# A Perceiver layer on one core: nine products of constants at the start, and three gate/up steps of the second half done inside the self attention

## The chip, the cores and the metric

The kernel runs on one core of a Trainium2 chip. The metric is the device time of one execution in microseconds; less is better. The engines are named as the profile names them: PE (TensorE, products), PEld (its weight loads), DVE (VectorE), ACT (ScalarE), POOL (GpSimd) and SP (SyncE, which here only issues DMAs). Each engine works through its own queue in order and waits on semaphores of others.

## The reference

A layer works on 16 sequences of 64 rows of 1024 numbers (1024 rows in all), with a context of 1024 rows for each sequence. In short:

```
x = x + cross_attention(layernorm(x), ctx)      # 32 heads of 32, 8 key/value heads, Wq Wk Wv Wo
x = x + self_attention(layernorm(x))            # rotary embedding, biases, no output weights
x = x + ffn(layernorm(x))

def ffn(x):
    xq = int4_quant(x)                          # per row: mean |x|, round, clip to -8..7
    gate, up = xq @ ternary(w_gate), xq @ ternary(w_up)     # 1024 -> 2752
    inter = int8_quant(up * relu(gate)**2)      # per row: max |.|, round
    return inter @ ternary(w_down)              # 2752 -> 1024
```

`ternary(w)` is -1, 0 or 1 times the mean of |w|, so each weight matrix must be read once for its mean and again to be rounded.

## The kernel before, in words

The 1024 rows make eight tiles of 128 rows, numbered 0 to 7 (two sequences each). Almost all of on-chip memory is one tile named `arena`, of which the code hands out places by hand: `place(kb, shape)` is a view that begins `kb` KB into each partition. The order of all instructions on all queues is the order of the Python code (`manual_schedule`); nothing is moved by a scheduler. Waits follow from the places and PSUM banks that instructions share.

**Start (lines 135 to 282).** Constants are made; then 8 chunks of the first context half are loaded on SP's queue (L266) and of the key/value weights on ACT's queue (L267). After them come the rows `x`, the second context half and the query weights. `project_first` (L584) multiplies chunk after chunk: for each chunk two key products of 512 columns (L590) and four value products of 256 columns (L598). Then follow the layer norms, transposes and query products (L360), and the first pass over the feed-forward weights.

**Cross attention (most of the time).** 32 units, two for each sequence. Products for the next sequence's keys and values (L497, L508) are cut into pieces and called between the steps of a unit: they are "fillers", a list from which `fill(n)` takes the next n entries. Context loads are released by the products that used their places before. Meanwhile all three feed-forward weight matrices pass through the core twice (L636, L644).

**Self attention (from L1464).** A loop over `t` = 0 to 8 handles tile `t` (called `two`) and the tile before it (`last`). For each tile: scores (`by_key`, L972), copies to memory (L982), row maxima on DVE (`maxima`, `row`) that go through a small DRAM buffer and come back on all partitions (L1012, L1016), subtraction (L1021), exponentials on ACT (L1024), values and sums on PE (`values`, L1032 and L1043), copies (L1051, L1054), transposes back (`finish`, L1064 and L1067), and the residual added on POOL (L1080). The scores of tile `t` and the values of tile `t` - 1 use the same four PSUM banks, `w`. Then comes the quantisation of the tile for the feed-forward part (`quantize`): statistics on DVE (L187), a power on POOL (L193), normalisation (L179), mean of |x| (L1113), rounding, and a transposing DMA on SP (L1125) that makes `xqT[t]`. `factors3` (L1131, L1132) makes the two factors of a tile on POOL.

**Gate/up steps.** The 2752 columns are cut into 8 chunks of 344. Step (n, t) multiplies tile t by gate and up chunk n (`gate_up`, L1144): 2 x 8 products of 128x344 (L1151) into two banks. Numbers 0 to 7 are the chunks for tiles 0 to 3 (the first half), 8 to 15 the same chunks again for tiles 4 to 7 (the second half); 64 steps in all. With `scalar=True` ACT does the relu, the scaled copy and the square (L1159, L1161, L1162), otherwise ACT does the relu and DVE a fused product (L1165); POOL makes the last product (L1163 or L1168). `fetch(n)` loads chunk n of both matrices into one of four pairs of places, for n < 4 on SP's queue, else on POOL's (L1141). Numbers from 8 on use the first three pairs only, since the fourth lies where tile 4's results are put.

While cross attention's leftovers last, the fillers of the self-attention loop are projections (`project2`, L252); from `t` = 4 on they are the 32 steps of the first half, as L1480 to L1491 order them. The second half (from L1535) is a plain list of steps with other work hung on to positions in it (`beside`): the down weights' load (`fetch_down`), the quantisation of tile 7, that of the results (`quantize8`), and the down products of tiles 0 and 1 (`down`, L1213). The remaining down products end the kernel.

Of the kernel before, what the change touches and what calls it, by code (L numbers as in the profile page):

```python
# [11 lines left out]
F32 = mybir.dt.float32  # L12
BF = mybir.dt.bfloat16
# [36 lines left out]
def kernel(  # L50
# [82 lines left out]


    ident = const.tile([P, P], F32, name="ident")
    make_identity(nc, ident)
# [8 lines left out]
    for g in range(2):  # L145
        nc.vector.memset(pick[:, g, g : g + 1], 1.0)
    minus = const.tile([P, P], BF, name="minus")
    nc.vector.memset(minus, -1.0)
    bq_sb = const.tile([P, 8], F32, name="bq_sb")
# [944 lines left out]
    ]  # L1094
    wb_pairs = [(112, 114.6875), (117.375, 120.0625), (91.25, 122.75), (0, 2.6875)]
    relu_ring = Ring(125.4375, 192.25, 199.625)
# [37 lines left out]
    def fetch(n):  # L1134

        wbs[n] = []
        pair = wb_pairs[n % 4] if n < NCH else wb_pairs[(n - NCH) % 3]
        for i in range(2):
            q = place(pair[i], [KC, CW], F8)
            queue = nc.sync if n < 4 else nc.gpsimd  # L1140
            queue.dma_start(q.rearrange("p k o -> p (k o)"), ternary[i][n % NCH])  # L1141
            wbs[n].append(q)
# [90 lines left out]
    with tc.manual_schedule():  # L1233
# [234 lines left out]
        fill(2)  # L1468
        two, last = None, None
        for t in range(NT + 1):  # L1470
            two, last = (Tile2(t, w) if t < NT else None), two
# [4 lines left out]
            if t == NT // 2:  # L1476
                fill(len(fillers))
                for n in (2, 3):
                    fetch(n)
                steps = [(n, tt) for n in range(NCH) for tt in range(NT // 2)]  # L1480

                steps[:12] = [
                    (n, tt) for tiles in ((0, 1), (2,), (3,)) for n in range(3) for tt in tiles
                ]

                def beside(n, tt):
                    gate_up(n, tt, lambda i: four_tile(f"gu_{n}_{tt}_{i}"), scalar=True)
                    if tt == NT // 2 - 1 and n + 4 < NCH + 3:
                        fetch(n + 4)

                fillers += [lambda s=s: beside(*s) for s in steps]  # L1491
# [6 lines left out]
            if t == NT // 2:  # L1498
                fill(2)
                last.exponentials()  # L1500
# [6 lines left out]
            if last and t != NT // 2:  # L1507
                last.exponentials()
                fill()

# [24 lines left out]
        pieces = quantize(NT - 1)  # L1535
        steps = [(n, t) for n in range(NCH, 2 * NCH) for t in range(NT // 2, NT)]

        steps[:12] = [s for s in steps[:12] if s[1] < NT - 1] + [s for s in steps[:12] if s[1] == NT - 1]
        beside = {9 + 2 * i: step for i, step in enumerate(sum(map(quantize8, range(4)), []))}
        beside[0] = fetch_down  # L1540
# [3 lines left out]
        for t in range(2):  # L1544
            beside[20 + 8 * t] = lambda t=t: (down(t, 0), down(t, 1))
        more = None
        for i, (n, t) in enumerate(steps):
            if i == 2:
                ps_w_closed.close()
                more = ctx.enter_context(tc.tile_pool(name="ps_g", bufs=4, space=PSUM))  # L1550
            if more:
                gate_up(n, t, lambda j: more.tile([P, 512], F32, tag="g", name=f"g_{n}_{t}_{j}"))
            else:
                gate_up(n, t, lambda j: four_tile(f"gu_{n}_{t}_{j}"))
            if i in beside:
                beside[i]()
            if t == NT - 1 and n + 3 < 2 * NCH:
                fetch(n + 3)
        for t in range(2, NT):
# [74 lines left out]
```

## Time and profile before

| what | value |
|---|---|
| median of three runs | 1798.24 us (1792.51, 1798.24, 1798.41) |
| profiled execution | 1793.57 us |
| its span | 1791.80 us |
| PE busy | 1746.8 us (97%) |
| DVE, ACT, POOL busy | 1270.0, 922.3, 946.6 us |
| self attention's second half (first step to tile 7's last transposes) | 1522.85 to 1633.31 us |

The span runs from the first to the last instruction of one execution; the time of the execution has some 1.8 us more. In a list of waits, a line gives the waiting engine and line of code, what ended the wait, the total, how many times, and the longest. In a timeline a row gives the start and the duration in microseconds from the span's start, the engine, the line, the operation, and `x4` for four instructions drawn together; rows of one engine may overlap a little, since the next instruction begins before the last one's results are out. A product of 32-bit numbers counts as two instructions. The brackets at the end of a row say how long the engine was idle before it and what released it.

### The profile page before, as it was taken

Reading aid. Unit: us, or ns where it says so; the run is one execution under the profiler, and the core shown is the slowest. Engines: PE = TensorE matmul, PEld = TensorE weight load, DVE = VectorE, ACT = ScalarE, POOL = GpSimd, SP = SyncE. Lnnn points to the kernel's source line nnn. Section 1 sums busy time; section 2 is a strip of 40 time slices with the busy share of each in tenths; the row PEclk is TensorE's granted clock in tenths of the full one; section 3 lists DMA queues with packets and bytes.
Section 4 is the critical chain, followed back from the end, with each engine's and each line's share of the span. In section 5 each row is a group of like instructions: output and inputs, shape, how many; then the busy total and the mean of one; then the engine's idle time right before and its main releaser. Section 6 shows DMA issues by size and latency. Waiting matters only on the chain.

```text
span 1791.8 us, 29303 instructions
## 1 busy us (share of the span) xinstructions
PE 1746.8 (97%) x12184; PEld 1119.1 (62%) x12184; DVE 1270.0 (71%) x1520; ACT 922.3 (51%) x1004; POOL 946.6 (53%) x564
## 2 busy tenths in 40 slices
PE   8999999999999999999999999999999999899999
PEld 5778566666667666666666666664446454566654
DVE  4343678778888888887888888889554258775564
ACT  1563566555777777776776775544201122564100
POOL 1000447576676676677577577576503433555530
PEclk9999999999999999999999999999999999999999
DMA  9575466557766776776785784551430024354534
GB/s 357 178 245 187 177 193 200 172 148 186 198 218 183 232 230 184 226 236 169 226 250 162 231 237 129 148 168 57 99 127 14 1 48 88 75 139 128 123 73 108
DMA packets 99093, 293.35 MB, mean 164 GB/s; under 512 B 41808, under 2 KB 50960, under 8 KB 84240
## 3 DMA queue, kind: packets, MB, share of 16 engines
q1 hardware_dynamic: 85232, 220.10, 36.4%
q0 software_dynamic: 12576, 69.28, 19.4%
q8 instruction: 96, 1.57, 0.4%
q10 hardware_dynamic: 1152, 2.10, 0.3%
q14 instruction: 37, 0.30, 0.1%
HBM read 264.38 MB, written 19.20 MB: 158 GB/s over the span
## 4 chain that ended last, share of the span: by engine, by line
PE 72%; DVE 12%; DMA 8%; ACT 3%; issue 2%; POOL 2%; SPq 0%; DVEq 0%; ACTq 0%; POOLq 0%
PE p L508 13%; PE p L497 12%; PE t L690 6%; PE o L752 6%; PE k L252 4%; PE q L252 4%; PE d L1213 4%; PE g L1151 4%; DVE arena L733 3%; DMA arena<-in_ctxT 3%; PE z L508 3%; PE wo L854 3%; PE q L360 3%; DVE arena L709 2%; PE v L421 2%; PE gu L1151 2%
## 5 line engine op out<-in xcount | busy, mean ns | idle before, releaser
L743 POOL TENSOR_TENSOR arena<-arena 128x1024 f32<-128x1024 f32 x188 | 497.7, 2647 | 72.7 <-ACT arena L734 62.2
L709 DVE TENSOR_TENSOR arena<-t,arena 128x512 f32<-128x512 f32 x384 | 261.2, 688 | 163.9 <-PE t L690 93.9
L733 DVE TENSOR_TENSOR arena<-arena 128x2048 f32<-128x2048 f32 x128 | 355.6, 2807 | 2.1 <-DMA arena<-tops 2.1
L734 ACT ACTIVATE arena<-arena 128x2048 f32<-128x2048 f32 x128 | 244.0, 1907 | 179.2 <-DVE arena L733 179.1
L508 PEld LDWEIGHTS p<-arena 128*128 128x128 f32 x2688 | 309.9, 192 | 34.0 <-issue 26.2
L702 ACT COPY arena<-t 128x1024 f32<-128x1024 f32 x256 | 253.1, 1009 | 137.4 <-DVE arena L706 61.7
L508 PE MATMUL p<-arena 128*128 128x128 f32 x2688 | 318.0, 277 | 0.0
L497 PE MATMUL p<-arena 128*128 128x512 f32 x672 | 309.4, 602 | 8.3 <-DMA arena<-in_ctxT 8.2
L497 PEld LDWEIGHTS p<-arena 128*128 128x128 f32 x672 | 122.1, 191 | 152.5 <-issue 136.5
L740 POOL TENSOR_TENSOR arena<-arena 128x1024 f32<-128x1024 f32 x32 | 77.4, 2417 | 262.5 <-ACT arena L734 180.9
L690 PE MATMUL t<-arena 32*128 32x256 f32 x2048 | 146.6, 400 | 2.8 <-DVE arena L709 2.5
L1151 PEld LDWEIGHTS <-arena 128*128 128x128 bf16 x1024 | 98.7, 97 | 58.7 <-issue 5.0
L690 PEld LDWEIGHTS t<-arena 32*128 32x128 f32 x2048 | 93.0, 184 | 61.3 <-issue 32.6
L752 PE MATMUL o<-arena 128*32 128x256 f32 x2048 | 123.8, 382 | 0.4 <-DVE wmean L653 0.4
L252 PE MATMUL q<-arena 128*128 128x512 f32 x256 | 112.2, 594 | 0.0
L854 PE MATMUL wo<-arena 128*128 128x512 f32 x224 | 100.5, 598 | 5.7 <-ACT arena L845 4.8
L360 PE MATMUL q<-arena 128*128 128x256 f32 x448 | 100.5, 382 | 3.1 <-ACT arena L371 1.7
L913 POOL TENSOR_TENSOR arena<-arena 128x512 f32<-128x512 f32 x20 | 33.5, 1672 | 118.3 <-DVE arena L911 118.3
L360 PEld LDWEIGHTS q<-arena 128*128 128x128 f32 x448 | 83.7, 190 | 18.2 <-ACT arena L371 4.0
L752 PEld LDWEIGHTS o<-arena 128*32 128x32 f32 x2048 | 60.2, 109 | 53.4 <-ACT arena L640 6.8
L477 POOL DMA_DIRECT2D arena<-in_ctxT x70 | 70.4, 1064 | 30.1 <-PE z L508 16.0
L1151 PE MATMUL gu<-arena 128*128 128x344 fp8e4 x544 | 83.3, 311 | 2.4 <-DMA arena<-arena 1.9
(156 smaller groups left out, 2318.4 us busy)
## 6 DMA issues: line engine op xcount, KB each, us to landing
arena<-in_ctxT SPq DMA_DIRECT2D x56, 1024.0 KB, 10.6
arena<-in_ctxT POOLq DMA_DIRECT2D x42, 1024.0 KB, 10.7
arena<-tops SPq DMA_DIRECT2D x48, 512.0 KB, 4.9
arena<-in_wg SPq DMA_DIRECT2D x32, 688.0 KB, 5.0
arena<-in_wu SPq DMA_DIRECT2D x32, 688.0 KB, 5.0
arena<-in_wd SPq DMA_DIRECT2D x32, 688.0 KB, 8.2
arena<-in_ctxT POOLq DMA_DIRECT2D x28, 512.0 KB, 8.7
ternary<-arena SPq DMA_DIRECT2D x48, 172.0 KB, 7.2
```

The costliest lines, as they stand in the source:

```text
L252: nc.tensor.matmul(made[0], lhsT=lhsT(k), rhs=rhs(k), start=(k == 0), stop=(k == KC - 1))
L360: nc.tensor.matmul(ps, lhsT=weights[:, k, :], rhs=what[:, k, :], start=(start and k == 0), stop=(k == 3), skip_group_check=True,)
L497: nc.tensor.matmul(ps, lhsT=weights[:, k, :], rhs=what[:, k, :], start=(first and k == 0), stop=(k == 3), skip_group_check=True,)
L508: nc.tensor.matmul(ps[:, bass.ts(kt, P)], lhsT=what[:, k, bass.ts(kt, P)], rhs=weights[:, k, :], start=(first and kt == 0 and k == 0), sto ...
L690: nc.tensor.matmul(ws[jj // 2][:, jj % 2, a, :], lhsT=self.kT[rows, self.g, bass.ts(i * 2 + a, P)], rhs=two_tiles[self.b // 2 % 2][rows, s ...
L702: nc.scalar.copy(pt[:, 2 * mine : 2 * mine + 2], ws[mine])
L709: nc.vector.tensor_tensor(m, w[:, :, a], m, ALU.max)
L733: nc.vector.tensor_tensor(pt, pt, by.to_broadcast([P, 4, 2, 256]), ALU.subtract)
L734: nc.scalar.activation(pt, pt, AF.Exp)
L743: nc.gpsimd.tensor_tensor(acc, acc, pt[:, :, a], ALU.add)
L752: nc.tensor.matmul(self.po[bass.ts(jj, HD), 0:256], lhsT=self.v[:, kt, bass.ts(self.g * 4 + jj, HD)], rhs=self.pts[i][:, jj, a, :], start= ...
L1151: nc.tensor.matmul(ps[:, :CW], lhsT=xqT[t][:, k, :], rhs=wbs[n][i][:, k, :], start=(k == 0), stop=(k == KC - 1),)
```

## The change

1. At the start, a place of 512 numbers of 16 bits is filled with ones on DVE, and PE multiplies it nine times into a bank that nobody reads. The constant `minus`, which no instruction read, and its memset are gone.
2. Steps (8, 4), (9, 4) and (8, 5) of the second half become the last three fillers of the self-attention loop (`ahead`), with `scalar=True`, and are taken out of the second half's list.
3. The loop asks for one more filler at three places: ahead of tile 3's exponentials, and after the exponentials at `t` = 5 and `t` = 8.
4. The order of the first 16 steps of the first half changes: chunk 3's steps for tiles 0 to 2 come before the four steps of tile 3, which before stood three places earlier.
5. Numbers 11 and 15 of the chunks get a fifth pair of places of their own (where `xqT` of tiles 0 to 3 lay), so that a chunk is fetched four numbers ahead instead of three in the second half; fetch 11 is now issued in the loop.
6. The positions in the second half's list move by three (`quantize8` from 9 to 6, down products from 20 to 17).

```diff
+    idle = place(200, [512], BF)
+    nc.vector.memset(idle, 1.0)
+    ps = t_tile([P, 512], F32, "idle")
+    for _ in range(9):
+        nc.tensor.matmul(ps, lhsT=idle[:, :P], rhs=idle, start=True, stop=True)
...
-    minus = const.tile([P, P], BF, name="minus")
-    nc.vector.memset(minus, -1.0)
...
-    wb_pairs = [(112, 114.6875), (117.375, 120.0625), (91.25, 122.75), (0, 2.6875)]
+    wb_pairs = [(112, 114.6875), (117.375, 120.0625), (91.25, 122.75), (0, 2.6875), (176, 193.75)]
...
-        pair = wb_pairs[n % 4] if n < NCH else wb_pairs[(n - NCH) % 3]
+        pair = wb_pairs[4 if n % 4 == 3 and n > NCH else n % 4]
...
+        ahead = [(NCH, NT // 2), (NCH + 1, NT // 2), (NCH, NT // 2 + 1)]
...
-                steps[:12] = [
-                    (n, tt) for tiles in ((0, 1), (2,), (3,)) for n in range(3) for tt in tiles
+                steps[:16] = [(n, tt) for tiles in ((0, 1), (2,)) for n in range(3) for tt in tiles] + [
+                    (3, 0), (3, 1), (3, 2), (0, 3), (1, 3), (2, 3), (3, 3)
                 ]
+                steps += ahead
...
-                    if tt == NT // 2 - 1 and n + 4 < NCH + 3:
+                    if tt == NT // 2 - 1:
                         fetch(n + 4)
...
             if t == NT // 2:
-                fill(2)
+                fill(3)
                 last.exponentials()
...
             if last and t != NT // 2:
                 last.exponentials()
-                fill()
+                fill(2 if t in (NT // 2 + 1, NT) else 1)
...
-        steps[:12] = [s for s in steps[:12] if s[1] < NT - 1] + [s for s in steps[:12] if s[1] == NT - 1]
-        beside = {9 + 2 * i: step for i, step in enumerate(sum(map(quantize8, range(4)), []))}
+        begun = [s for s in steps[:16] if s not in ahead]
+        steps[:16] = [s for s in begun if s[1] < NT - 1] + [s for s in begun if s[1] == NT - 1]
+        beside = {6 + 2 * i: step for i, step in enumerate(sum(map(quantize8, range(4)), []))}
...
-            beside[20 + 8 * t] = lambda t=t: (down(t, 0), down(t, 1))
+            beside[17 + 8 * t] = lambda t=t: (down(t, 0), down(t, 1))
...
-            if t == NT - 1 and n + 3 < 2 * NCH:
-                fetch(n + 3)
+            if t == NT - 1 and n + 4 < 2 * NCH:
+                fetch(n + 4)
```

## The prediction

> **What bounds the kernel now.** I read the page first: TensorE is busy for 97% of the span, so time can only be won where TensorE is idle or runs at half clock, or where its work gets shorter. No useful product is removed here, so I looked for idle and slow places with the list of waits and the timeline, at the two places that the change touches.
>
> ```profile
> PE 1746.8 (97%) x12184; PEld 1119.1 (62%) x12184; DVE 1270.0 (71%) x1520; ACT 922.3 (51%) x1004; POOL 946.6 (53%) x564
> ```
>
> At the start (timeline, TensorE; columns: start, duration, instruction):
>
> ```profile
> 0.96 0.17 DVE L148 MEMSET minus<- 128x128 bf16 x1
> 5.73 3.75 PE L590 MATMUL k_first<-arena 128*128 128x512 f32 x4 [5.73 <-DMA arena<-in_ctxT]
> 9.27 2.96 PE L598 MATMUL v_first<-arena 128*128 128x256 f32 x8
> 12.07 1.88 PE L590 MATMUL k_first<-arena 128*128 128x512 f32 x4
> 13.79 1.89 PE L598 MATMUL v_first<-arena 128*128 128x256 f32 x8
> 15.52 1.02 PE L590 MATMUL k_first<-arena 128*128 128x512 f32 x2
> ```
>
> The first load lands at 5.7 us. The first chunk of products then takes 12.07 - 5.73 = 6.34 us, the second, of the same form, 15.52 - 12.07 = 3.45 us, with no wait between them. So TensorE begins at half speed and loses 2.89 us. The granted clock has no entry that early; the durations show it.
>
> In the self attention, the waits of TensorE from 1520 to 1640 us (waiting line, what it waited for, total, times, longest):
>
> ```profile
> PE w L1032 <- ACT arena L1024: 6.2, 4, 2.8
> PE w L972 <- POOL arena L914: 2.5, 1, 2.5
> PE gu L1151 <- DMA arena<-arena: 1.9, 1, 1.9
> PE gu L1151 <- DMA arena<-ternary: 0.5, 1, 0.5
> ```
>
> That is 11.1 us of idle, and after the long waits the clock drops too (timeline of TensorE; 1557 and 1626 against 1604):
>
> ```profile
> 1557.53 1.91 PE L1032 MATMUL w<-arena 64*32 64x256 f32 x32 [2.81 <-ACT arena L1024]
> 1559.13 2.01 PE L1043 MATMUL w<-arena,pick 64*32 64x256 f32 x32
> ...
> 1604.11 1.10 PE L1032 MATMUL w<-arena 64*32 64x256 f32 x32 [0.52 <-ACT arena L1024]
> 1605.00 1.07 PE L1043 MATMUL w<-arena,pick 64*32 64x256 f32 x32
> ...
> 1626.25 1.96 PE L1032 MATMUL w<-arena 64*32 64x256 f32 x32 [2.32 <-ACT arena L1024]
> 1627.96 1.75 PE L1043 MATMUL w<-arena,pick 64*32 64x256 f32 x32
> 1629.64 2.52 PE L1151 MATMUL gu<-arena 128*128 128x344 fp8e4 x16
> ```
>
> The value products take 1.90 us at 1604 and 3.4 to 3.6 us after the waits of 2.3 and 2.8 us. After 1640 TensorE waits 0.5 us in all:
>
> ```profile
> PE d L1213 <- DVE arena L1220: 0.3, 1, 0.3
> PE g L1151 <- DMA arena<-ternary: 0.2, 1, 0.2
> ```
>
> So the end is set by two things: when tile 7's last transposes (L1067) end, 1633.31 here, and how many of the 64 gate/up steps are still to do then (31 are done, 33 left).
>
> **Prices, all from start to start.** A gate/up step: four take 1588.17 to 1597.66, 2.37 each. Scores L972: 1.05 (1597.66 to 1598.71). Values L1032 and L1043: 1.90 (1604.11 to 1606.01). Transposes L1064 and L1067: 1.30 (1608.37 to 1609.67).
>
> **Part 1, the nine products on ones.** They need only VectorE's memset of 128x512 bf16. The removed memset of a quarter of that took 0.17 us; the new one costs 0.2 to 0.7, ahead of memsets that nobody waits for before 11 us. TensorE can begin near 1.4. The trace has no such product; the down products L1213, also 512 wide, take 9.50/44 = 0.216 each at full clock (1685.32 to 1694.82), twice that at half: nine last 3.9 us and end near 5.3, before the load at 5.73. They delay nothing. How soon the clock rises is bounded by the slow spells: after the waits above they last 3.4 us (1626.25 to 1629.64) and 3.6 us, at the start 5.7. By 5.73 TensorE has been at work for 4.3 us with a gap of some 0.4. If 3.6 us suffice, all 2.9 us are won; if it takes 5.7, then 1.4 us stay slow and lose 0.7, so 2.2 are won; if the gap starts the count afresh, nothing. I take 2.5. The cover behind it: chunks 2 to 8 follow without a wait, the window from 10 to 20 us moves 409 GB/s against the 0.5 MB per 3.45 us that they need, and tiles 0 to 3 are normalised well before their transposes (39.61 us). After that loads are released by consumption, so the lead stays; five waits on context loads (8.2 us in all) may shift by 1 or 2 us either way.
>
> The Trainium skill, "TensorE: Matmul & The Clock Gate", Part 1, speaks against this: the clock rises after one busy window of about 3.4 us, and the windows run freely. Read strictly, nine products of 3.9 us hold a whole window in one case of seven, for an expected 0.4 us in place of 2.5, and a sum of 8.0. The trace is milder: the products that began at 1626.25 were back at full clock at 1629.64, 3.4 us later, and a window that had to be full and could begin anywhere would make that luck.
>
> **Part 2, the steps.** Three steps of chunks 8 and 9 (tiles 4, 4, 5) move ahead of tile 7's transposes, one step stands before tile 4's scores, tile 3's steps (the fourth tile) come after chunk 3's first three, and fetches move with their steps. Time and steps done, before from the trace, after worked below:
>
> | point | before | after |
> |---|---|---|
> | tile 4 scores begin | 1527.64, 2 | 1530.0, 3 |
> | tile 3 values begin | 1535.40, 3 | 1536.8, 4 |
> | tile 5 scores begin | 1548.80, 7 | 1552.4, 8 |
> | tile 4 values begin | 1557.53, 9 | 1560.6, 11 |
> | tile 6 scores begin | 1576.16, 14 | 1575.7, 16 |
> | tile 5 values begin | 1582.61, 16 | 1582.7, 18 |
> | tile 6 values begin | 1604.11, 23 | 1604.9, 25 |
> | tile 7 values begin | 1626.25, 30 | 1627.2, 33 |
> | tile 7 transposes end | 1633.31, 31 | 1632.8, 34 |
>
> Step (1,0) fills most of the 2.50 us wait for POOL's L914. But its three ScalarE evictions (0.44 apart) now stand before tile 3's exponentials and the copies L982 that free the score banks. These ended at 1535.34 and now end at 1536.8. TensorE, done with (1,1) at 1533.7, waits 3.1 us there, then runs the values slowly (3.6), and waits until 1541.66 for the fetch of chunk 2, whose place on SP's queue, behind tile 2's transpose (L1125, 1536.85), is unchanged. So the early gain is lost again. From there TensorE has (2,0), tile 3's transposes, (2,1), (0,2), (1,2), tile 5's scores, (2,2), (3,0), (3,1) without a wait: 7 x 2.37 + 1.30 + 1.05 = 18.9, to 1560.6. Tile 4's exponentials must be ready then. Tile 3's transposes end at 1545.3; the residual add L1080 ends 4.4 later as at 1566.67 to 1571.05, at 1549.7. POOL's power L193 is now behind the product of (0,2), until 1553.1. Then norm and L1113 (2.5), L1021 (2.3), exponentials (1.9): 1559.9. The wait of 2.81, its slow 1.7 and the 1.86 for tile 3's transposed copy (now landed at 1565.4, wanted at 1566.2) go.
>
> For tiles 5 to 7 VectorE and POOL set the pace, 21.5 us a tile in the trace (1582.61 to 1604.11), against 7 x 2.37 + 4.25 = 20.8 of TensorE. There the order on POOL's queue counts, since L193 waits in it:
>
> ```profile
> 1596.19 0.56 POOL L193 TENSOR_TENSOR rs_n<-ve_n,neg_half 128x1 f32<-128x1 f32 x1
> 1596.72 0.90 POOL L1163 TENSOR_TENSOR arena<-arena 128x344 f32<-128x344 f32 x1
> 1596.79 1.39 DVE L179 TENSOR_SCALAR arena<-arena,mv_n,rs_n 128x1024 f32<-128x1024 f32 x1 [0.84 <-POOL rs_n L193]
> 1597.58 1.27 POOL L1141 DMA_DIRECT2D arena<-ternary  x2
> ```
>
> Tile 4's L193 is behind two fetches instead of three but starts later: exponentials at 1582.6, as before. Tile 5's and tile 6's now stand behind the fetches of chunks 8 and 10 (1.27 and 1.15 of POOL). That makes tile 6's values 0.8 later and tile 7's chain 1.9; but tile 7 had waited 1.03 for its maxima anyway, so 0.95 later, 1627.2. TensorE arrives with its eight steps at 1604.9 + 1.90 + 8 x 2.37 + 1.30 = 1627.1, so it runs on at full clock: 1627.2 + 1.90 + 2.37 + 1.30 = 1632.8. Fetch 4 has three steps less of lead, but is wanted near 1576.7 and issued near 1572; the nearest row took 3.1 us from issue to use (1661.02 to 1664.17). Fetch 11 moves to before tile 7's values, to a free pair of places. The three moved steps evict through ScalarE alone, two instructions of 0.44 us each in place of VectorE's L1165 (0.57); ScalarE is busy for 13.8 of 20 us in that stretch and four banks take turns, so I cost this at nothing. Down weights are issued on SP when tile 7's values are done, as at 1628.39. Behind 1633 the order is the old one counted from tile 7's transposes: its rounded copy six steps after them, its first step ten, the first down product as many steps after tile 0's maximum. Gain: 3 x 2.37 + 0.5 = 7.6. Bounds: if POOL products in these four iterations are stretched as the one at 1553.47 is (2.83 in place of 0.91), 4 x 1.9 = 7.7 is lost, a gain of 0; if the fetches cost POOL nothing on the chain, 8.5. Nearest to the ordinary rows, I keep 7.6.
>
> **Sum.** 2.5 + 7.6 = 10.1 us. The profiled execution took 1793.57 (span 1791.80 and 1.77 around it), 4.7 below the median of the three runs, which ended at 1792.5, 1798.2 and 1798.4. That gives 1783.5 against it and 1788.1 against the median; since two of the three were near 1798, I say 1787.0. About 0.5%, 9 us, is what a measurement of this kernel can tell from no change.
>
> **Rivals.** A: VectorE and POOL give it back. If L193 comes 1.2 us later at each of four tiles (a fetch that stands in front of it each time), tile 7's values come 4.8 later than I work out: sum 2.5 + 2.8 = 5.3, about 1793 against the median. For it: the chain has only 0.5 us of slack a tile. Against: only two of the four fetches moved in front. B: the products at the start win nothing, because of the gap at 5.3 or because the five waits on context loads grow by as much: sum 7.6, 1790.6. C, slower: a lead of 2.5 us makes TensorE meet the context loads (L497) earlier than they land. The longest such wait is 2.4 us, and a slow spell costs some 1.7 more; there are 13 batches. Three batches with 4.1 us each would undo the whole gain, five would make it slower by over 0.5%, about 1808. Against it: the loads are released by TensorE's own progress, so they move with it.
>
> **How the numbers follow.** My forecast 0.57 (0.49 with over 9 us, 0.08 just under), A 0.22, B 0.13, C 0.08. Faster 0.49, within 0.43, slower 0.08. The range from 1780, both terms at their upper bounds against the quicker runs, to 1797, rival A with nothing from the start against the median. My forecast alone: 1782 to 1790.
>
> **What would show it.** Right: the first L590 row near 5.7 with 1.9 us for four, all 8 first chunks at 3.45; tile 7's values with a wait under 1 us and 1.9 us long; 30 steps after tile 7's transposes; waits of 3 us for L982 and for the fetch of chunk 2 newly there. Wrong: a first chunk of over 5 us; waits on L1024 of over 2 us at tiles 5 to 7; context waits of over 12 us.

## The result, and the profile after

The changed kernel is slower: 1802.68 us (median of 9 runs, 1797.31 to 1811.46) against 1795.65 us (9 runs, 1792.51 to 1798.55) of the kernel before beside it, a ratio of 1.0034 with a 95% interval of 1.0018 to 1.0050 (the ratio is not formed from the two medians, whose quotient is 1.0039). Of the runs below, two of the kernel with the steps alone, 1813.82 and 1819.84 us, lie more than 1.5% above the quickest of that kernel and are left out of its ratio. The profiled execution took 1803.24 us, its span is 1801.4 us, 9.6 more than the span before. The lines of the code that the views name stand three lower than before, from the constants on (L590 is L593 now, L1213 is L1216).

The busy times (page of the changed kernel) hardly tell it, TensorE being 4.0 us busier (its weight loads 2.9) and the other engines within 1.3:

```profile
PE 1750.8 (97%) x12193; PEld 1122.0 (62%) x12193; DVE 1270.3 (71%) x1517; ACT 923.6 (51%) x1010; POOL 947.3 (53%) x564
```

The start, timeline of TensorE after (start, duration, instruction, idle before it):

```profile
1.46 4.02 PE L139 MATMUL idle<-arena 128*128 128x512 bf16 x9 [1.46 <-DVE arena L136]
5.84 2.51 PE L593 MATMUL k_first<-arena 128*128 128x512 f32 x4 [0.35 <-DMA arena<-in_ctxT]
8.18 1.89 PE L601 MATMUL v_first<-arena 128*128 128x256 f32 x8
9.90 1.88 PE L593 MATMUL k_first<-arena 128*128 128x512 f32 x4
```

The first chunk now takes 9.90 - 5.84 = 4.06 us instead of 6.34, and where the second chunk begins the kernel is 2.17 us ahead.

The self attention, waits of TensorE from 1520 to 1640 us after (waiting line, what it waited for, total, times, longest), and rows of its timeline there:

```profile
PE w L1035 <- ACT arena L985: 2.8, 1, 2.8
PE gu L1154 <- DMA arena<-ternary: 2.1, 2, 1.2
PE w L1035 <- ACT arena L1027: 2.0, 2, 1.2
```

```profile
1539.58 1.96 PE L1035 MATMUL w<-arena 64*32 64x256 f32 x32 [2.81 <-ACT arena L985]
...
1563.35 1.09 PE L1035 MATMUL w<-arena 64*32 64x256 f32 x32
...
1630.33 1.09 PE L1035 MATMUL w<-arena 64*32 64x256 f32 x32
1631.21 1.07 PE L1046 MATMUL w<-arena,pick 64*32 64x256 f32 x32
1632.22 2.52 PE L1154 MATMUL gu<-arena 128*128 128x344 fp8e4 x16
```

11.1 us of waits have become 6.9. Tile 4's and tile 7's values come without a wait and at full clock (1.09 instead of 1.91 and 1.96). New are tile 3's wait for the copies, 2.81 us, and a wait of 0.88 us for a fetch at 1580.39; the one for chunk 2's fetch has grown from 0.53 to 1.17 us. After 1640 us something else is new (waits of TensorE to the end, and its timeline):

```profile
PE d L1216 <- DMA arena<-arena: 11.8, 1, 11.8
PE g L1154 <- DMA arena<-ternary: 0.7, 1, 0.7
PE d L1216 <- DVE arena L1223: 0.3, 1, 0.3
```

```profile
1642.93 36.56 PE L1154 MATMUL g<-arena 128*128 128x344 fp8e4 x248
1680.18 1.35 PE L1154 MATMUL g<-arena 128*128 128x344 fp8e4 x8 [0.69 <-DMA arena<-ternary]
1693.34 11.23 PE L1216 MATMUL d<-arena 128*128 128x512 fp8e4 x44 [11.80 <-DMA arena<-arena]
1704.40 0.90 PE L1154 MATMUL g<-arena 128*128 128x344 fp8e4 x5
```

The first down product of tile 0 needs the tile's result, rounded and transposed by a DMA on SP's queue (the last line of `quantize8`, L1195). It waits 11.80 us for it, and then runs part of its way at half clock: 1704.40 - 1693.34 = 11.06 us instead of 9.50. Before, the same product had no wait:

```profile
1685.32 9.66 PE L1213 MATMUL d<-arena 128*128 128x512 fp8e4 x44
```

The time, stretch by stretch, from these timelines:

| stretch | before | after | difference |
|---|---|---|---|
| start: lead at the second chunk | 0 | 2.17 ahead | -2.17 |
| to the last projection product | ends 1522.85 | ends 1525.65 | +4.97 (the lead lost, and 2.80 more) |
| to tile 7's last transposes | 1633.31 | 1635.88 | -0.23 |
| three steps fewer left behind them | 33 | 30 | -7.11 (3 x 2.37) |
| behind 1633.31 and 1635.88, less these steps | 158.49 | 165.52 + 7.11 | +14.14 |

The sum is +9.6. Of the last row, 11.80 is the wait, 1.56 the half clock behind it and 0.69 a fetch.

What went wrong with that DMA is seen in the views of DMA issues (window 1655 to 1700 us; number, size, median from issue to landing), first before, then after:

```profile
arena<-ternary POOLq DMA_DIRECT2D x10, 344.0 KB, 3.8
out<-arena SPq DMA_DIRECT2D x2, 256.0 KB, 3.5
arena<-arena SPq DMA_TRANSPOSE x2, 7.3
```

```profile
arena<-ternary POOLq DMA_DIRECT2D x8, 344.0 KB, 16.3
arena<-arena SPq DMA_TRANSPOSE x2, 19.8
```

In a window around its issue alone, tile 0's transposing DMA took 5.4 us to land before and 25.6 us after:

```profile
arena<-arena SPq DMA_TRANSPOSE x1, 5.4
```

```profile
arena<-arena SPq DMA_TRANSPOSE x1, 25.6
```

Both it and the weight fetches beside it became four to five times slower. Their issues, POOL's timeline and SP's (the transposing DMAs of tiles 0 and 1 are drawn together as x2, so the row begins with tile 0's; a fetch is two DMAs, the second issued some 0.6 us after the first). Before:

```profile
1661.02 1.16 POOL L1141 DMA_DIRECT2D arena<-ternary  x2
1664.86 2.16 POOL L1141 DMA_DIRECT2D arena<-ternary  x2
1667.89 1.11 POOL L1141 DMA_DIRECT2D arena<-ternary  x2
1675.39 1.11 POOL L1141 DMA_DIRECT2D arena<-ternary  x2
```

```profile
1672.30 18.64 SPq L1192 DMA_TRANSPOSE arena<-arena  x2
```

After:

```profile
1664.05 2.51 POOL L1144 DMA_DIRECT2D arena<-ternary  x2
1667.52 1.11 POOL L1144 DMA_DIRECT2D arena<-ternary  x2
1669.50 1.11 POOL L1144 DMA_DIRECT2D arena<-ternary  x2
1671.48 1.11 POOL L1144 DMA_DIRECT2D arena<-ternary  x2
```

```profile
1667.62 25.84 SPq L1195 DMA_TRANSPOSE arena<-arena  x2
```

Fetches of four consecutive chunks (12 to 15) hang on four consecutive steps, (8,7), (9,7), (10,7) and (11,7), and the transposing DMA is now issued between the second and the third of them, 0.10 us behind the second (and so ahead of that fetch's own second DMA). Before, it was issued 4.41 us behind the third of three fetches and 3.09 us ahead of the next.

### The profile page after: what moved, and what is told of

Read it like the earlier page. It is cut to its first block, busy times and chain, and to the rows that moved or that the text cites. A ratio compares the mean times of both kernels' runs of the same rounds, so it can differ in the third digit from the quotient of the medians.

```text
span 1801.4 us, 29319 instructions
## 1 busy us (share of the span) xinstructions
PE 1750.8 (97%) x12193; PEld 1122.0 (62%) x12193; DVE 1270.3 (71%) x1517; ACT 923.6 (51%) x1010; POOL 947.3 (53%) x564
## 4 chain that ended last, share of the span: by engine, by line
PE 72%; DVE 12%; DMA 7%; issue 3%; ACT 3%; POOL 3%; POOLq 0%; ACTq 0%; DVEq 0%
PE p L511 14%; PE p L500 13%; PE t L693 6%; PE o L755 6%; PE k L255 4%; PE q L255 4%; PE d L1216 4%; DVE arena L736 3%; DMA arena<-in_ctxT 3%; PE z L511 3%; PE q L363 3%; PE g L1154 3%; PE wo L857 3%; DVE arena L712 2%; PE v L424 2%
## 5 line engine op out<-in xcount | busy, mean ns | idle before, releaser
L916 POOL TENSOR_TENSOR arena<-arena 128x512 f32<-128x512 f32 x20 | 33.4, 1672 | 118.3 <-DVE arena L914 118.3
L1154 PE MATMUL gu<-arena 128*128 128x344 fp8e4 x592 | 89.5, 309 | 2.1 <-DMA arena<-ternary 2.1
L1216 PE MATMUL d<-arena 128*128 128x512 fp8e4 x352 | 78.2, 385 | 12.1 <-DMA arena<-arena 11.8
```

The lines of the kernel that those rows point to most:

```text
L1154: nc.tensor.matmul(ps[:, :CW], lhsT=xqT[t][:, k, :], rhs=wbs[n][i][:, k, :], start=(k == 0), stop=(k == KC - 1),)
```

## Experiments

All were run beside the kernel before on the same chip; ratios are to it, with 95% intervals. "The changed kernel" is the one of the diff above. None of the kernels leaves out any of the computation.

### Each part alone

The start alone: the kernel before with the nine products and without `minus`. The steps alone: the changed kernel without the nine products.

```
     # e1: the kernel before, and
+    idle = place(200, [512], BF)
+    nc.vector.memset(idle, 1.0)
+    ps = t_tile([P, 512], F32, "idle")
+    for _ in range(9):
+        nc.tensor.matmul(ps, lhsT=idle[:, :P], rhs=idle, start=True, stop=True)
     # e2: the changed kernel without these five lines, with minus
```

> The kernel before with the nine products of ones (and without the unread constant), no step moved. In the changed kernel the first chunk of products took 4.06 us in place of 6.34 and the lead stood at 2.7 us up to 300 us; at 314 it was 0.5 and at 1270 a lag of 2.7. Theory A (the lead itself makes the context loads come late): the same loss shows here, the projections of the second half end 2 to 4 us later than before although the start is 2.2 us earlier, the ratio is 1.001 to 1.003. Theory B (the waits on context loads scatter from execution to execution): the lead is somewhere between kept and lost, the waits on context loads lie between 6 and 14 us, and over the rounds the kernel is 1 to 2.5 us faster, ratio 0.9985 to 0.9995. No wait at the first down product in either.

> The changed kernel without the nine products. The first down product waited 11.8 us for the transposed copy of tile 0 in the changed kernel. Theory (crowded DMA: the transposing DMA of tile 0 shares the DMA engines with the fetches of chunks 12 to 15, which the change issues within 8 us of each other): that wait is here too, 9 to 14 us, with a slow spell of TensorE; 34 steps are done when tile 7's transposes end; ratio 1.003 to 1.006. Rival (the wait hangs on the time that the nine products gained, or on that one execution): the wait is under 3 us, and the ratio 0.995 to 0.997.

Measured: the start alone 1795.6 us (12 runs), ratio 0.9995 [0.9979, 1.0010]; the steps alone 1803.75 us (12 runs), 1.0022 [0.9997, 1.0047], with single runs from 1787.0 to 1819.84; the ratio is below the 1.003 to 1.006 that I expected and not clear of 1. The start's profile is 2.87 us ahead at 20 us and 1.1 us behind at 1470 us: the lead is won and is not there at the end; that is less than theory A's lag of 2 to 4 us, and the ratio lies at the edge of theory B's range. The steps alone have the same slow tail, so it belongs to them and not to the products (TensorE's timeline, steps alone):

```profile
1685.90 2.47 PE L1151 MATMUL g<-arena 128*128 128x344 fp8e4 x8 [5.73 <-DMA arena<-ternary]
1697.27 11.14 PE L1213 MATMUL d<-arena 128*128 128x512 fp8e4 x44 [8.90 <-DMA arena<-arena]
```

### Taking the fetches away from the rounding, or the rounding from the fetches

```
     # e3: the changed kernel; fetches 14 and 15 later
-            if t == NT - 1 and n + 4 < 2 * NCH:
+            if t == NT - 1 and n + 4 < 2 * NCH - 2:
                 fetch(n + 4)
+            if i in (14, 19):
+                fetch(14 + (i == 19))
     # e4: the changed kernel; tile 0's maximum, scaling and rounding after steps 5, 6, 8 (were 6, 8, 10)
-        beside = {6 + 2 * i: step for i, step in enumerate(sum(map(quantize8, range(4)), []))}
+        early = (5, 6, 8)
+        beside = {early[i] if i < 3 else 6 + 2 * i: step for i, step in enumerate(sum(map(quantize8, range(4)), []))}
```

> The changed kernel with the fetches of chunks 14 and 15 held back: issued after steps (12,5) and (13,6) in place of (10,7) and (11,7), so that two fetches and not four stand beside tile 0's transposing DMA. Crowded DMA: that DMA lands 4 to 10 us sooner, the wait at the first down product falls from 11.8 to under 4 us, and the kernel is 8 to 13 us faster than the changed one, 1789 to 1794. Rival (the transposing DMA is slow by itself because it is issued at a bad place on SP, or because of the fetches 12 and 13 directly around it): the wait stays above 8 us and the time at 1800 to 1803.

> The changed kernel with tile 0's quantisation moved up: maximum, scaling and rounding after steps (11,4)-1, (11,4) and (11,6) in place of (11,4), (11,6) and (9,7), so that its transposing DMA is issued two steps, 4.7 us, before the fetch of chunk 12 has been asked for. Crowded DMA: it is through, or nearly, when the fetches come: it lands within 8 to 12 us of its issue, no wait of over 1 us at the first down product, the fetches land in 4 to 8 us, and the time is 1786 to 1790, a ratio of 0.993 to 0.997. Rival (what is short is only the number of steps between the copy and its use): the wait falls by the 4.7 us alone, to about 7, time about 1796.

Measured: 1789.3 us, ratio 0.9968 [0.9949, 0.9986], and 1789.88 us, 0.9966 [0.9949, 0.9983]. In both the wait is gone (TensorE's timeline, the held fetches first, then the early rounding), and the transposing DMA of tile 0 lands in 13.6 and 7.8 us:

```profile
1679.73 1.35 PE L1154 MATMUL g<-arena 128*128 128x344 fp8e4 x8 [0.78 <-DMA arena<-ternary]
1680.92 9.66 PE L1216 MATMUL d<-arena 128*128 128x512 fp8e4 x44
```

```profile
1671.72 12.20 PE L1154 MATMUL g<-arena 128*128 128x344 fp8e4 x80 [0.58 <-DMA arena<-ternary]
1683.76 9.66 PE L1216 MATMUL d<-arena 128*128 128x512 fp8e4 x44
```

Either repair turns a loss of some 6 us into a gain of some 6. Both kernels beat the kernel before and the changed one.

### Both repairs, with and without the products; the down products later

```
     # e5: the changed kernel with early = (5, 6, 8), and fetches 14 and 15 after steps 13 and 18
     # e7: e3 without the five lines of the nine products
     # e9: e5 without them
     # e12: the changed kernel
-            beside[17 + 8 * t] = lambda t=t: (down(t, 0), down(t, 1))
+            beside[19 + 8 * t] = lambda t=t: (down(t, 0), down(t, 1))
```

> The changed kernel with both repairs at once: the maximum, scaling and rounding of tile 0's result stand after steps 5, 6 and 8 (of the second half's last loop) instead of 6, 8 and 10, and the fetches of chunks 14 and 15 are issued after steps 13 and 18 instead of with the last steps of chunks 10 and 11. Nothing of the computation changes. If the transposing DMA of the rounded result was late because four fetches fell beside it, each repair alone had already freed the first down product of its wait, so both together can add little: the transposing DMA lands in 5 to 8 us, no wait at the first down product, 1787 to 1790 us, ratio to the kernel before 0.994 to 0.997. If the fetches themselves are what costs time (each repair left a fetch wait of 0.6 to 0.8 us), both together win about 1 us more. If the gain of the two repairs came from the shift of the order against something else, both together may lie anywhere, and a wait of several us would show at a down product or a fetch.

> The repaired kernel whose fetches of chunks 14 and 15 are held back (ratio 0.9968 to the kernel before), without the nine products of ones at the start. Theory that the lead of the start is given back at the context loads near 305 to 320 us: the start is 2.2 to 2.9 us later, the wait on the context load near 308 us is 1.7 to 3.1 us instead of 4.5 to 4.7 and its loss of 2.4 us is gone, and the time is the same within 0.5 us; ratio 0.996 to 0.998. Theory that the lead is kept and only scattered waits hide it: 2.2 to 2.9 us slower, ratio 0.9983 or above.

> The changed kernel with both repairs (rounding of tile 0's result after steps 5, 6 and 8; fetches 14 and 15 held to steps 13 and 18) and without the nine products of ones. Theory that the products are worth nothing over the whole kernel, because their 2.5 us are given back before 1500 us: as the same kernel with them, ratio to the kernel before 0.9935 to 0.9975, 1786 to 1790 us. Theory that the start's gain is kept: 2.5 us slower than with them, ratio 0.997 or above.

> The changed kernel with only the down products of tiles 0 and 1 two steps later (after steps 19 and 27 instead of 17 and 25); fetches and rounding stay. Crowding theory: the transposing DMA of tile 0's result still takes 20 to 26 us beside its four fetches, but two steps (4.7 us) more lie before the first down product, which waits about 7 us instead of 11.8: 4 to 6 us faster than the changed kernel, ratio to the kernel before 0.9995 to 1.002. Rival (the wait belongs to what the down product itself needs at that place, weights or banks): it still waits 9 to 12 us, ratio 1.002 to 1.005.

Measured: both repairs 1789.29 us, 0.9955 [0.9936, 0.9974], the transposing DMA in 7.7 us, no wait at the first down product, a fetch wait of 0.57: nothing is added to what one repair gives. Without the products, the held fetches took 1788.44 us, 0.9955 [0.9938, 0.9973], where they had 0.9968 with them; both repairs took 1790.45 us, 0.9973 [0.9958, 0.9987], where they had 0.9955. Once the products lose 0.0013 and once they win 0.0018: over the whole kernel no gain of theirs is seen, within some 3 us.

With the down products two steps later, the transposing DMA is as slow as in the changed kernel (23.9 us) and the first down product still waits, 6.25 us, about what 11.80 less two steps leaves (7.06):

```profile
1687.26 11.67 PE L1216 MATMUL d<-arena 128*128 128x512 fp8e4 x44 [6.25 <-DMA arena<-arena]
```

That confirms that the DMA lands at its own time, whoever asks for it. The kernel's time, 1794.04 us and 0.9979 [0.9960, 0.9998], is better than I expected (0.9995 to 1.002). In its profile the code ahead of 1500 us, which is the same as in the changed kernel, ran 5.9 us quicker (at 1470 us it was 3.07 ahead of the kernel before, the changed kernel 2.80 behind); so that much two executions of the same code can differ there.

### The kernel before with the rounding moved into the fetches

```
     # e6: the kernel before
-        beside = {9 + 2 * i: step for i, step in enumerate(sum(map(quantize8, range(4)), []))}
+        beside = {(6 if i < 3 else 9) + 2 * i: step for i, step in enumerate(sum(map(quantize8, range(4)), []))}
```

> The kernel before, with only the maximum, scaling and rounding of tile 0's result three steps earlier (after steps 6, 8 and 10 of the last loop instead of 9, 11 and 13); the first down product stays at step 20. Crowding theory: the rounding now falls between the fetches of chunks 11 to 13, so its transposing DMA lands in 12 to 20 us instead of 5.4, and the fetches beside it in 6 to 16 us instead of 3.8; ten steps (about 23.7 us) lie before the first down product, so it waits little or not at all, a fetch may be waited for by 1 to 6 us, and the ratio is 1.000 to 1.004. Rival (the transposing DMA was late in the changed kernel for another reason, as the tables of places or the steps moved): it lands in 5 to 7 us, and the time is that of before, ratio 0.999 to 1.001.

Measured: 1802.36 us, 1.0032 [1.0014, 1.0049]. The transposing DMA took 19.3 us instead of 5.4, the fetches 8.0 at the median instead of 3.8. The down product, ten steps later, did not wait; TensorE waited three times for fetches:

```profile
1666.19 1.35 PE L1151 MATMUL g<-arena 128*128 128x344 fp8e4 x8 [0.62 <-DMA arena<-ternary]
1668.39 9.57 PE L1151 MATMUL g<-arena 128*128 128x344 fp8e4 x64 [0.85 <-DMA arena<-ternary]
1678.43 10.74 PE L1151 MATMUL g<-arena 128*128 128x344 fp8e4 x72 [0.47 <-DMA arena<-ternary]
```

So the place of the rounding alone, in a kernel that has none of the change's other parts, makes the DMA slow. In this profile, which is of the quickest of the ten runs, the tail lost 2.9 us (span 3.7 longer, 0.75 of it ahead of 1470 us); the rest of the 6 us between the medians is not explained by it.

### Number of fetches, or their order

By then the landing times did not fit a mere count of the fetches beside it: with the early rounding four fetches follow within 7.7 us of the issue, and it lands in 7.8. Two more kernels separate the count from the order.

```
     # e13: the changed kernel; fetch 13 one step later, with fetch 14
             if t == NT - 1 and n + 4 < 2 * NCH:
-                fetch(n + 4)
+                if n + 4 == 14:
+                    fetch(13)
+                if n + 4 != 13:
+                    fetch(n + 4)
     # e14: the kernel e4 with the rounding one step later
-        early = (5, 6, 8)
+        early = (5, 6, 9)
```

> The changed kernel with only fetch 13 one step later (issued just ahead of fetch 14), so that no fetch is issued in the microsecond ahead of the transposing DMA of tile 0's result; three fetches now follow it within about 5 us. Order theory (the transposing DMA is slowed by a fetch issued just ahead of it or together with it, and each further fetch adds some 6 us only then): it lands in 6 to 10 us, no wait at the first down product, 1788 to 1791 us, ratio to the kernel before 0.995 to 0.998. Number theory (each fetch that falls beside it adds some 6 us, wherever it stands): still three to four fetches, 19 to 26 us, a wait of 5 to 12 us at the first down product, ratio 1.000 to 1.004.

> The kernel with the early rounding (maximum, scaling and rounding of tile 0's result after steps 5, 6 and 8), with only the rounding one step later, after step 9, where fetch 12 is issued too. The same four fetches fall beside the transposing DMA, but one is now issued just ahead of it. Order theory: it lands in 13 to 28 us instead of 7.8, and the first down product, eight steps (19 us) later, waits 0 to 9 us; ratio 0.997 to 1.003. Number theory (four fetches beside it both times): 7 to 9 us as with the rounding after step 8, no wait, ratio 0.995 to 0.998.

Measured: fetch 13 behind the transposing DMA: 1789.08 us, 0.9952 [0.9936, 0.9967], landing in 9.7 us, no wait. Rounding after step 9: 1793.85 us, 0.9979 [0.9967, 0.9990], landing in 13.3 us, no wait at the down product, but one of 4.30 us for a fetch. TensorE's rows, first fetch 13 behind, then rounding after step 9:

```profile
1680.77 9.66 PE L1216 MATMUL d<-arena 128*128 128x512 fp8e4 x44
```

```profile
1673.51 13.41 PE L1154 MATMUL g<-arena 128*128 128x344 fp8e4 x72 [4.30 <-DMA arena<-ternary]
1686.77 9.66 PE L1216 MATMUL d<-arena 128*128 128x512 fp8e4 x44
```

What the order theory expected came in both, what the number theory expected in neither. The transposing DMAs of tile 0's result together (issue times of each fetch's first DMA relative to its own, from the timelines of POOL and SP; the kernels that change the start alone are as the kernel before, 5.2 to 5.3 us):

| kernel | fetches ahead, us | fetches behind, us | landing, us |
|---|---|---|---|
| before | 4.41 | 3.09 | 5.4 |
| both repairs, with and without products | none near | 1.06, 3.09 | 7.7, 7.7 |
| early rounding | none near | 1.06, 3.09, 5.30, 7.65 | 7.8 |
| fetch 13 behind | 3.57 | 0.79 (two), 3.83 | 9.7 |
| rounding after step 9 | 0.09 | 1.93, 3.93, 5.91 | 13.3 |
| held fetches, with and without products | 3.57, 0.10 | 9.01 | 13.6, 10.2 |
| before, rounding moved | 3.56, 0.10 | 1.88, 11.82 | 19.3 |
| down products later | 3.56, 0.10 | 1.89, 3.87 | 23.9 |
| changed | 3.57, 0.10 | 1.88, 3.86 | 25.6 |
| steps alone | 3.58, 0.11 | 1.88, 3.86 | 28.8 |

With no fetch issued just ahead it lands in 5.4 to 9.7 us, however many follow 0.8 us or more behind. With one 0.1 us ahead and none following within 9 us it takes 10.2 and 13.6 us, and with others following closely 13.3 to 28.8. Tile 1's transposing DMA in the kernel before, 0.09 us behind fetch 15 with no other near, took 9.3 us (8.9 to 9.3 in the five other kernels that issue it so). So what makes it slow is a fetch issued within about half a microsecond of it, and further fetches add to that, save with the rounding after step 9, where three behind cost less than two elsewhere; there none stands 3.6 us ahead. Whether it is the fetch's first DMA, 0.1 us ahead, or its second, issued 0.46 to 0.51 us behind the transposing DMA in all these kernels, no run separates; the first landed in 3.7 to 4.5 us in all of them, the second in 8.8 to 17.1. In no kernel does a fetch begin between 0.11 and 3.56 us ahead of tile 0's transposing DMA.

The DMA views show more (packets, their bytes and mean rate, how many are small; then for each queue packets, MB and the time of its packets as a share of the 16 engines). In the changed kernel the packets of the two queues (small ones of the transposing DMA on `hardware_dynamic`, large ones of the fetches on `software_dynamic`) run mixed, and both together move 100 GB/s (window 1671 to 1681 us):

```profile
DMA packets 2304, 1.00 MB, mean 100 GB/s; under 512 B 2225, under 2 KB 2225, under 8 KB 2304
q1 hardware_dynamic: 2208, 0.57, 92.1%
q0 software_dynamic: 96, 0.43, 36.3%
```

With fetch 13 behind they run one after the other, first the transposing DMA (1669 to 1672 us), then the fetches (1674 to 1679 us):

```profile
DMA packets 2117, 0.54 MB, mean 180 GB/s; under 512 B 2117, under 2 KB 2117, under 8 KB 2117
```

```profile
DMA packets 562, 1.89 MB, mean 379 GB/s; under 512 B 225, under 2 KB 225, under 8 KB 560
```

So both are slow while their packets are mixed. With the early rounding, too, they run apart (198 GB/s from 1667 to 1670 us, 398 from 1673 to 1677), and with the rounding after step 9, 0.45 of the transposing DMA's 0.72 MB went through from 1667 to 1669 us, before the slow stretch. Why mixed packets move so slowly, and why a fetch so close makes them mix, no run here shows.

### More products at the start

To see what becomes of the start's lead, the kernel before was given more products: 18, 26, or 13 in 32 bits of 256 columns (the profile counts two for each of those, so 26 again).

```
-    for _ in range(9):
+    for _ in range(18):      # e10; 26 in e8
     # e11: [256] of F32 for idle, range(13), into ps[:, :256]
```

> The kernel before with 26 products of ones at the start instead of none: they end near 9.8 us, so the first load's products begin about 4 us late but at full clock, and the first projection stage ends some 1 us later than in the kernel before. Theory that TensorE's lead is given back at the context loads near 308 us because the loads land at their own time: without a lead the wait there is 1.7 to 2.5 us as before (4.5 us with a lead of 2.7 to 3.2) and the lag of 1 us shrinks to 0 to 0.5 us behind 320 us; time as before, ratio 0.999 to 1.001. Theory that the wait there has nothing to do with the lead: 1.9 to 4.7 us by chance, and the lag of 1 us is kept on average, ratio 1.0005.

> The kernel before with 18 products of ones instead of 9 or 26. They end near 7 us, and at 20 us the kernel is about 1.6 us ahead of the kernel before (2.9 with nine, 0.0 with 26). Theory that only the lead is given back: time as before, ratio 0.999 to 1.001. Theory that the products past the ninth have a cost of their own (26 were 1.0028, 5.2 us, with no lag at 300 us): about half of it, ratio 1.001 to 1.0025. If neither (chance of how the later waits fall): any ratio from 0.999 to 1.003.

> The kernel before with 13 products of ones in float32, 128x256, in place of none: half as many instructions as the 26, and, estimated at four passes each, about as long, so they end between 8 and 10 us and the lag at 20 us is 0 to 1.2 us. If the 5.2 us that 26 products cost came from the number of instructions before the first load's products, about a half of it or less is left, ratio 1.000 to 1.0015. If it came from when the first products begin, or from TensorE being at work for those 9 us, the ratio is 1.002 to 1.004.

Measured: 18 products 1796.76 us, 1.0005 [0.9991, 1.0019]; 26 products 1801.54 us, 1.0028 [1.0012, 1.0045]; 13 in 32 bits 1803.09 us, 1.0046 [1.0030, 1.0062]. The 18 fall into the range of the first theory; the 13 in 32 bits are slower than either of theirs. Since the last make as many instructions as the 26, they do not tell the number from the duration, as they were meant to. How far each kernel is ahead of the profile before (minus) or behind (plus), from the starts of the same products, one execution each, in us:

| kernels | at 20 us | at 270 us | at 320 us | at 1470 us |
|---|---|---|---|---|
| no products (e2, e6, e7, e9) | 0.0, -0.8, -0.5, -0.1 | 3.0, 1.9, 0.3, 0.8 | 2.5, 1.6, 0.1, 0.7 | 0.8, 0.8, 1.3, 0.7 |
| nine: changed, e1, e3, e4 | -2.2, -2.9, -2.7, -2.4 | -2.7, -3.2, -0.2, -2.8 | -0.2, -0.9, -2.1, -0.2 | 2.8, 1.1, 0.2, 3.0 |
| nine: e5, e12, e13, e14 | -2.5, -2.6, -1.8, -0.6 | -3.3, -2.6, -2.3, -1.1 | -1.8, -3.5, 0.1, -0.4 | 2.1, -3.1, 1.3, -0.1 |
| 18 (e10) | -1.7 | -1.4 | 0.9 | 4.6 |
| 26 (e8) | 0.1 | 0.0 | 0.7 | 7.8 |
| 13 in 32 bits (e11) | 0.7 | 0.7 | 2.8 | 9.8 |

The eight executions with nine products are 2.2 us ahead at 20 us on the mean and 0.9 behind at 1470 us; the four without products end 0.9 behind too. So the lead is gone before the self attention, on the mean of single executions that differ by up to 6 us there. Against the mean of the four, the eight are ahead by 1.9 us at 20 us, 3.8 at 270, 2.3 at 320 and nothing at 1470. One place where it goes is at the context loads near 308 us. Before, and with nine products in the changed kernel (TensorE's timeline):

```profile
308.46 5.71 PE L497 MATMUL p<-arena 128*128 128x512 f32 x8 [1.86 <-DMA arena<-in_ctxT]
```

```profile
305.26 1.98 PE L500 MATMUL p<-arena 128*128 128x512 f32 x4 [1.39 <-DMA arena<-in_ctxT]
310.31 3.40 PE L500 MATMUL p<-arena 128*128 128x512 f32 x4 [3.07 <-DMA arena<-in_ctxT]
```

The changed kernel comes to the first load earlier, but waits 1.39 and 3.07 us and runs part of the second four at half clock: 2.5 us of its 2.7 are gone behind it. Six of the seven executions that came there 1 us or more ahead with nine products, and the one with 18, lost 0.7 to 2.5 us at it. The seventh (the late down products) lost nothing: the same load let its second four begin at 308.70 us. (The one that came there with a lead of only 0.15, the held fetches, gained 2.0.) So the load's landing varies, and with a lead there is mostly a wait for it. The stretch from 270 to 320 us takes 1.5 of the 3.8 us; the other 2.3 are lost behind it, at places that were not followed. That 26 products, neither ahead nor behind at 270 us, then lose 7.8 us by 1470 us and 5 us in the medians is explained by neither theory; the losses are steps of 0.3 to 2 us, waits and stretches at half clock, spread from 360 to 1280 us. This is left open.

## Why the prediction was wrong

**Start, 2.5 us: right at the start, wrong in its cover.** 2.17 us were won at the second chunk, and in the eight executions 0.6 to 2.9. The clock rose 5.5 us after the first product on ones in the changed kernel (1.46 to about 6.95, from the first chunk's durations), about 3.4 us after it with 26 products in a row (26 in 7.31 us are 8 at 0.43 and 18 at 0.22), and with the rounding after step 9, where the gap ahead of the first chunk was 0.63 us, only some 8.5 us after it: there all key products of the first chunk were still slow (3.54 us, as before). The Trainium skill, "TensorE: Matmul & The Clock Gate", Part 1, has the window run freely, so that the same kernel starts with a different number of slow products each time; these executions agree with that, while my estimate of 0.4 us from its strict reading was too little. What failed is the statement "After that loads are released by consumption, so the lead stays". It did not stay; the start alone is worth 0.9995 [0.9979, 1.0010]. Rival B named this outcome for the start, "because the five waits on context loads grow by as much": from 100 to 1500 us they grew from 8.2 to 9.9, so they are a part of it only. Of the 4.97 us lost there in this pair of profiles, 2.17 are the lead; the other 2.80 are within what identical code differs by (5.9 us).

**Steps, 7.6 us: right where I followed them.** With the 2.80 us that the stage began late taken off, tile 4's scores begin at 1529.99 (I had 1530.0), tile 7's transposes end at 1633.08 (1632.8), and 34 steps are done. The new wait for the copies (L985) is 2.81 us where I had 3.1. The wait at tile 7's values is gone. Not foreseen was the wait of 0.88 us for fetch 4, which took 5.1 and 5.4 us from issue to landing where I had taken 3.1 from another row; tile 7's values still come within 0.4 us of what I had. With the tail repaired, six kernels lie at 0.9952 to 0.9973, some 5 to 9 us faster, with the products and without: about the steps' worth.

**The tail, costed at nothing: this step failed.** It was the sentence "Behind 1633 the order is the old one counted from tile 7's transposes: its rounded copy six steps after them, its first step ten, the first down product as many steps after tile 0's maximum." Of the steps this is true: from the rounding (after step 13 in the kernel before, 10 in the changed one) to the down product (20 and 17) there are seven in both. But I counted steps alone. Fetches hang on steps too, on those of tile 7, and these begin behind nine others in both kernels. Part 6 of the change moved the rounding from behind them into their midst, 0.10 us behind a fetch, and part 5, the distance of four, made the fetches four in a row instead of three. So the order was not the old one. That the move of the rounding alone makes the DMA slow is shown by the kernel before with the rounding moved (19.3 us). The cover of seven steps, 16.6 us, was ample for the 5.4 us of the trace and not for 25.6. I had followed POOL's queue fetch by fetch in the self attention, where L193 waits in it, and not here, where the fetches meet another queue's DMA. That put the sum wrong by 14.1 us in this pair of profiles.

**The rivals.** Neither A nor C came. C, the slower one, expected its loss at the context loads, some 20 us; the loss came in the tail, from a mechanism that I had not listed. The trace of before held a warning that I passed over: tile 1's transposing DMA, issued together with fetch 15, took 9.3 us against 5.2 to 6.9 of the others. The ends of my range are rounded outward from their sums: 1792.5 less 2.9 and 8.5 is 1781.1, and 1798.2 less 2.8 is 1795.4.

## What to carry to other kernels

When steps are moved, line up every queue behind them anew, not only the engines: list each DMA that hangs on a step and see which other transfers it now is issued next to. A DMA that lands in 5 us alone may need 25 beside others, as here, so the cover of a late consumer has to be measured against the crowded time, or the issues set apart; here one step's delay of one fetch was worth some 14 us (1.0034 against 0.9952). And a lead won at the start of a long kernel counts at the end only if waits in the middle are shown not to take it back.

## What was not expected of the hardware

- A transposing DMA on SP's queue that lands in 5.2 to 5.4 us alone took 8.9 to 28.8 us with a weight fetch begun 0.1 us ahead of it on POOL's queue, and in the changed kernel the fetches took up to 21 us (16.3 at the median) instead of 3.8. While their packets ran mixed, both together moved 100 GB/s; one after the other they moved 180 and 379. Issued 1.06 us ahead of the first of four fetches, it took 7.8 us and the fetches 5.6.
- The Trainium skill, "Advanced Engine Details and Errata", section "X-Bar Transpose (TRN2)", calls transposing DMAs as fast as regular ones. Alone that is near to what is seen here (5.2 us for a rounded tile, 3.8 for one DMA of a fetch, 344 KB). Mixed with fetches, transposing and regular DMA are slow alike (25.6 and up to 21 us), so the sentence gives no measure of how long a transposing DMA takes there.
- Many products on ones were followed by losses long after them. With 26 ahead of the first load the kernel was even with the one before at 270 us and 5.2 us slower at the end (1.0028 [1.0012, 1.0045]), with 18 no loss is seen in the times (1.0005 [0.9991, 1.0019]); why is open.
